# A perceiver block on one core: the steady stage's matmuls in four 64x64 quarters, half sums joined on the way out of PSUM, division behind the Wv products

## The chip, the core and the metric

The kernel runs on one core of a Trainium2 chip. The core has a TensorE (PE in the profile; its weight loads are PEld), a VectorE (DVE), a ScalarE (ACT), a GpSimd (POOL) and a SyncE (SP), which here only issues transfers. Each engine works through its own instructions in a fixed order and waits on semaphores for the others. The metric is the device time in microseconds (us) of one execution, the median of the runs shown. All data is float32.

## The reference, cut to what matters

```python
x = x + xattn(layernorm(x), ctx)      # x: 32 x 64 x 256,  ctx: 32 x 1601 x 192
x = x + time_mixing(layernorm(x))     # a scan over the 64 steps
x = x + ffn(layernorm(x))             # relu, width 1024

def xattn(query, context):            # 16 heads of 64
    q = query @ w_q;  k, v = split(context @ w_kv)
    attn = softmax(q k^T / 8)         # per batch and head, 64 x 1601
    return (attn @ v) @ w_out + b_out

def time_mixing(x):
    k, v, r = ...                     # three 256x256 products of mixes of x and x shifted by a step
    num, den = scans with decay td    # out_t = (num + e v) / (den + e)
    return (sigmoid(r) * out) @ Wo + bo
```

## The kernel before, in words

**Folding.** Keys and values are never formed. A setup stage multiplies each head's query with that head's key weights, so that a query becomes a vector of 192 numbers that is matched with the context itself; the folded queries go to DRAM (`q_dram`) and come back batch by batch. The other way round, the softmax weights are multiplied with the context, which gives 192 numbers per query and head, and only then with the head's value weights (`vproj`, the Wv products) and with `w_out` (`yproj`).

**Units.** The steady stage is the loop `for u in range(2 * B)` over 64 units; a unit is one batch and 8 of its 16 heads, so 8 x 64 = 512 columns. The 1601 keys are 12 chunks of 128, a rest of 64, and one odd key that is treated apart (`odd_pd`, `odd_u`, `share`). For unit u the loop does, in program order:

1. `scores(u)`: six pairs of chunks. The contraction of 192 is cut in three steps of 64 rows, and the two chunks of a pair sit in the upper and the lower 64 rows of the array (L658, form 64*128), each with a PSUM bank of its own. ACT copies each pair to `s_sb` (L665), DVE keeps a running maximum `m` (L667 to L677). For even u, the rest's scores (`rest_scores`, L635) come behind the first pair.
2. `max_all`: POOL's all-reduce over the partitions gives `mb` (L684).
3. For the unit before, u-1: `av_lo` (L468), the weights times the context's first 128 channels, two instructions side by side in the two 64-column halves of the array, and `av_hi` (L864), the last 64 channels. `left` (L809, L819) adds the rest's 64 keys in forms of 64*128. During `av_lo` the queue takes in the `fill` of the unit's phase.
4. `exps(u)`: DVE subtracts `mb` (L692, three L703), ACT exponentiates (L693, three L704).
5. `total(u-1)`, which program order puts ahead of `scores(u)`: DVE sums the exponentials (L766 to L770), POOL all-reduces the sum over the partitions to `den` (L772). `inverse`: DVE turns it (L784), takes the reciprocal of 16 numbers per partition (L786) and turns it back to full width, `rden` (L788, in the buffer of `den`).
6. `before.out()`, for u-2: DVE multiplies `o_lo` and `o_hi` from PSUM with `rden` into `oT_lo` (L885) and `oT_hi` (two L890 of 64 partitions).

**Phases.** Four units are two batches, 128 rows of `x_sb`. So work that belongs to 128 rows goes by the phase (u-5) % 4: phase 0 does `vproj` (L919, L933) behind `av_hi`, and the mixing's `scan` (DVE: eight L575, then L580, L583, a reciprocal L586, L588); phase 1 `yproj` and the mixing's `out` as fills of `av_lo`, and `norm`, whose square root is a POOL power (L111); phase 2 `mix` (transposes L514; ACT and DVE take turns on L523 and L526); phase 3 `project` (Wk, Wv) and `gate` (Wr). In phases 0 and 2 DVE also turns the next batch's context (L372, L373).

**PSUM.** `ps_s` holds two pairs of banks for scores, `ps_o` one bank each for `o_lo` and `o_hi`, `ps_m` two banks for all else. So scores wait for nothing but ACT's copy of the pair two before, and `o_lo` and `o_hi` may stay in their banks until the next unit's `av_lo`.

**Order.** Each engine's order is fixed when the program is built; `tc.issue_after` ties some of it. After the loop there are the last unit, the last mixing and four blocks of the feed-forward net (`ffn`).

Of the kernel before, what the change touches and what calls it, by code (L numbers as in the profile page):

```python
# [9 lines left out]
F32 = mybir.dt.float32  # L10
# [10 lines left out]
def kernel(  # L21
# [51 lines left out]
    ODD = C2 + H  # L73
# [21 lines left out]
    bias_rows = const.tile([P, 3, D], F32, name="bias_rows")  # L95
# [7 lines left out]
    rows = [const.tile([P, 3, P], F32, name=f"rows_{k}") for k in range(2)]  # L103
    odd_pd = const.tile([ODD, 2, P], F32, name="odd_pd")
    odd_u = const.tile([ODD, D], F32, name="odd_u")
    for t in rows + [odd_pd, odd_u]:
        nc.gpsimd.memset(t, 0.0)
# [18 lines left out]
    with ExitStack() as st_b:  # L126
        with ExitStack() as st_a:
# [20 lines left out]
            def rows_load(b):  # L148

                for r0 in (0, C2):  # L150
                    for n, cs in ((0, slice(0, P)), (1, slice(P, C))):
                        nc.sync.dma_start(
                            rows[b % 2][r0 : r0 + KR, n, n * C2 : P], ctx_768[b, KC * P : NK - 1, cs]
                        )
# [282 lines left out]
            def late_loads():  # L437
# [11 lines left out]
                for n, v in enumerate((b_out, bo, b2)):  # L449
                    nc.sync.dma_start(bias_rows[:, n, :], v.partition_broadcast(P))  # L450
                with nc.allow_non_contiguous_dma(reason="per-channel vectors"):
                    for n, v in enumerate((time_decay, time_first)):
                        nc.sync.dma_start(cols[:, n, :], v.rearrange("(c p) -> p c", p=P))
                    for n, v in enumerate((mix_k, mix_v, mix_r)):
                        nc.sync.dma_start(
                            cols[:, 2 + n, :], v.rearrange("a b (c p) -> p (a b c)", p=P)
                        )
                    nc.sync.dma_start(b1_sb, b1.rearrange("(c p) -> p c", p=P))

            ps_m = st_b.enter_context(tc.tile_pool(name="ps_m", bufs=2, space=PSUM))  # L460
            ps_s = st_a.enter_context(tc.tile_pool(name="ps_s", bufs=2, space=PSUM))
            ps_o = st_a.enter_context(tc.tile_pool(name="ps_o", bufs=1, space=PSUM))

            def matmul(out, lhsT, rhs, start, stop):
# [7 lines left out]
                return last  # L472

# [22 lines left out]
            class Mixing:  # L496
# [13 lines left out]
                def mix(self):  # L510
                    i = self.i
                    pt = bank([P, 2, 2, T], f"xT_ln2_{i}")
                    for c in range(2):
                        nc.tensor.transpose(pt[:, c, :, :], self.xn[:, c * P : (c + 1) * P], ident)  # L514
                    xp = rp.tile([P, 2, 2, T + 1], F32, tag="xp", name=f"xp_{i}")
                    nc.gpsimd.memset(xp[:, :, :, 0:1], 0.0)
                    nc.scalar.copy(xp[:, :, :, 1 : T + 1], pt)
# [14 lines left out]
                def proj(self, n, w):  # L532
                    ps = bank([P, 2, 2, T], f"{w}_ps_{self.i}")
# [11 lines left out]
                def project(self):  # L545
# [3 lines left out]
                    pv = self.proj(1, "Wv")  # L549
                    self.ek = rp.tile(shape, F32, tag="in_k", name=f"ek_{i}")  # L550
# [9 lines left out]
                    self.values = nc.vector.tensor_tensor(self.ev, self.e, pv, ALU.mult)  # L560
                def gate(self):
                    i = self.i
                    pr = self.proj(2, "Wr")
# [29 lines left out]
                def out(self):  # L593
                    i = self.i
                    py = bank([P, D], f"ry_{i}")
                    for c in range(2):
                        matmul(
                            py,
                            lhsT=self.rw[:, c, :],
                            rhs=rw_T["Wo"][:, c, :],  # L600
                            start=(c == 0),
                            stop=(c == 1),
                        )
                    nc.vector.tensor_tensor(x_sb[:, i, :], x_sb[:, i, :], py, ALU.add)
                    nc.vector.tensor_tensor(
                        x_sb[:, i, :], x_sb[:, i, :], bias_rows[:, 1, :], ALU.add
                    )

            def rest_scores(b, cT, q):
# [8 lines left out]
                for j in range(2):  # L618
                    rest = ap.tile([P, 2, HH], F32, tag="rest", name=f"rest_{b}_{j}", bufs=3)
                    for o in range(2):  # L620
                        r0 = (1 - o) * KR
                        h0 = j * NP + o * NP // 2
                        nc.gpsimd.memset(rest[r0 : r0 + KR, o, :], LOW)  # L623
                        nc.sync.dma_start(
                            rest[r0 : r0 + 1, o, :].rearrange("p (h t) -> p h t", t=T),
                            o_dram[b // QB][h0 : h0 + NP // 2, k, k * T : (k + 1) * T].unsqueeze(0),
                        )
                    rests.append(rest)
                ps = ps_s.tile([P, 2, HALF], F32, tag="s", name=f"rest_ps_{b}")
                for s in range(NS):  # L630
                    for j in range(2):
                        rs = slice(j * C2, (j + 1) * C2)
                        for o in range(2):
                            n0 = j * HALF + o * HH
                            nc.tensor.matmul(  # L635
                                ps[o * KR : (o + 1) * KR, j, 0:HH],
                                lhsT=cT[rs, s, NB1 * BL : KT],
                                rhs=q[rs, s, n0 : n0 + HH],
# [4 lines left out]
                for j in range(2):  # L643
                    for o in range(2):
                        rs = slice(o * KR, (o + 1) * KR)
                        nc.scalar.copy(rests[j][rs, o, :], ps[rs, j, 0:HH])
                return [r.rearrange("p o n -> p (o n)") for r in rests]

            def scores(u, cT, q, hooks):
# [3 lines left out]
                for i in range(KC // 2):  # L653
                    ps = ps_s.tile([P, 2, HALF], F32, tag="s", name=f"s_ps_{u}_{i}")
                    for s in range(NS):
                        for k in range(2):
                            rs = slice(k * C2, (k + 1) * C2)
                            done = nc.tensor.matmul(  # L658
                                ps[:, k, :],
                                lhsT=cT[rs, s, i * P : (i + 1) * P],  # L660
                                rhs=q[rs, s, js : js + HALF],
                                start=(s == 0),
                                stop=(s == NS - 1),
                            )
# [5 lines left out]
                    if i == 4:  # L670
                        nc.vector.tensor_tensor(m2[:, 1, :], m2[:, 1, :], rests[u % 2], ALU.max)
# [15 lines left out]
            def exps(u, s_sb, rest, mb):  # L687
# [3 lines left out]
                def left():  # L691
                    nc.vector.tensor_tensor(rest, rest, mb, ALU.subtract)  # L692
                    nc.scalar.activation(rest, rest, AF.Exp)  # L693
                    for o in range(2):
                        r, h0 = (1 - o) * KR, j * NP + o * NP // 2
                        nc.scalar.dma_start(
                            pd_dram[b, 0, h0 : h0 + NP // 2].rearrange("h t -> (h t)").unsqueeze(0),
                            rest[r : r + 1, o * HH : (o + 1) * HH],
# [49 lines left out]
            class Half:  # L748
# [14 lines left out]
                def total(self):  # L763
                    u, p = self.u, self.s_sb
                    t2 = aw.tile([P, 2, HALF], F32, tag="t2", name=f"t2_{u}")
                    nc.vector.tensor_tensor(t2, p[:, 0:2, :], p[:, 2:4, :], ALU.add)  # L766
                    nc.vector.tensor_tensor(t2[:, 0, :], t2[:, 0, :], self.rest, ALU.add)
                    for i in range(2, KC // 2):
                        nc.vector.tensor_tensor(t2, t2, p[:, 2 * i : 2 * i + 2, :], ALU.add)  # L769
# [6 lines left out]
                def inverse(self):  # L776
# [5 lines left out]
                    u = self.u  # L782
                    turned = aw.tile([P, HALF // BL, BL], F32, tag="turned", name=f"turned_{u}")
                    nc.vector.transpose(turned, self.den.rearrange("p (k q) -> p k q", q=BL))  # L784
                    few = aw.tile([P, HALF // BL], F32, tag="few", name=f"few_{u}")
                    nc.vector.reciprocal(few, turned[:, :, 0])  # L786
                    self.rden = aw.tile([P, HALF // BL, BL], F32, tag="den", name=f"rden_{u}")
                    nc.vector.transpose(  # L788
                        self.rden, few.unsqueeze(2).to_broadcast([P, HALF // BL, BL])
                    )  # L790

                def keep(self):
# [3 lines left out]
                        self.rden.rearrange("p k q -> p (k q)")[0:1],  # L796
                    )

# [431 lines left out]
```

## Time and profile before

| | us |
|---|---|
| median of 3 runs (lowest, highest) | 2552.46 (2551.37, 2556.37) |
| the profiled execution, span from first to last instruction | 2552.2 |
| first score matmul of a unit to the next one's, phases 0, 1, 2, 3 | 34.93, 38.55, 32.66, 36.42 |
| busy: PE, DVE, ACT, POOL | 2531.5, 1929.0, 982.0, 411.2 |
| scores L658; `o_lo` L468; `o_hi` L864 (busy) | 1008.1; 679.1; 337.0 |
| rest into `o_lo` L809; into `o_hi` L819 (busy) | 81.1; 81.1 |

The span of the profiled execution stands 0.3 us under the median, so that differences against either are the same. In the tables, a row such as "64*128 64x512" is a matmul with 64 rows and 128 columns of the array in use, and 512 columns streamed through 64 partitions. A float32 matmul stands in the trace as two instructions, so counts there are twice those in the code. Four units, phases 0 to 3, are called a cycle here; in the middle of the run a cycle takes 142.56 us.

### The profile page before, as it was taken

The page shows a single profiled execution, that of the slowest core. Times are in us where ns is not written, and L with a number is a line of the kernel's source. Part 1 is how long each engine was busy: PE and PEld are TensorE (multiplying, and loading weights), DVE is VectorE, ACT ScalarE, POOL GpSimd, SP SyncE. Part 2 cuts the span into 40 slices and gives each one's busy share as a digit, 9 for nine tenths or more (in the row PEclk, how much of TensorE's full clock was granted, in tenths as well). Part 3 has the DMA queues.
Part 4 walks back from the last instruction along what each step waited for, and adds up shares of the span by engine and source line. Part 5 has one row for each costly group of instructions (what it writes and reads, how often), then busy time and mean ns, then how long its engine had stood idle before and what let it go on. Part 6 is the DMA issues. An engine that isn't in the chain of part 4 may idle for free.

```text
span 2552.2 us, 38114 instructions
## 1 busy us (share of the span) xinstructions
PE 2531.5 (99%) x15594; PEld 1213.1 (48%) x15594; DVE 1929.0 (76%) x2370; ACT 982.0 (38%) x1097; POOL 411.2 (16%) x372
## 2 busy tenths in 40 slices
PE   9989999999999999999999999999999999999999
PEld 3334444444444444444444454444444444444466
DVE  5377878878787878878787878878787878877741
ACT  3343434434333434434333444343443344343321
POOL 1002111111111121111111111111111111111100
PEclk9999999999999999999999999999999999999999
DMA  8787333333232223233332323233332323310111
GB/s 197 219 211 115 60 67 55 59 66 65 57 66 58 51 55 66 48 66 66 63 62 60 59 42 66 48 66 66 66 66 53 67 41 59 60 34 21 53 46 37
DMA packets 450223, 177.37 MB, mean 69 GB/s; under 512 B 347680, under 2 KB 435776, under 8 KB 450048
## 3 DMA queue, kind: packets, MB, share of 16 engines
q1 hardware_dynamic: 449664, 174.68, 33.5%
q8 instruction: 122, 2.00, 0.4%
q14 instruction: 53, 0.43, 0.1%
q10 hardware_dynamic: 384, 0.26, 0.0%
HBM read 142.64 MB, written 30.67 MB: 68 GB/s over the span
## 4 chain that ended last, share of the span: by engine, by line
PE 92%; DVE 4%; issue 1%; DMA 1%; POOL 1%; ACT 1%; SPq 0%; DVEq 0%; ACTq 0%; POOLq 0%
PE s_ps L658 36%; PE o_lo L468 24%; PE o_hi L864 12%; PE y_ps L468 2%; PE q_ps L292 2%; PE h_ps L1134 2%; PE fy L1150 2%; PE rest_ps L635 2%; PE o_hi L819 1%; PE v_ps L919 1%; PE ql_ps L313 1%; DVE s_sb L703 1%; PE o_lo L809 1%; DVE m L669 1%; PE v_ps L933 1%
## 5 line engine op out<-in xcount | busy, mean ns | idle before, releaser
L658 PE MATMUL s_ps<-q,cT 64*128 64x512 f32 x4608 | 1008.1, 590 | 1.8 <-ACT q_hi L350 0.8
L658 PEld LDWEIGHTS s_ps<-q,cT 64*128 64x128 f32 x4608 | 443.5, 187 | 516.0 <-issue 497.7
L468 PE MATMUL o_lo<-s_sb,c 128*64 128x512 f32 x3024 | 679.1, 596 | 5.9 <-DMA c<-in_ctx_dram 5.9
L665 ACT COPY s_sb<-s_ps 128x1024 f32<-128x1024 f32 x384 | 388.3, 1011 | 739.5 <-PE s_ps L658 731.4
L703 DVE TENSOR_TENSOR s_sb<-s_sb,mb 128x2048 f32<-128x2048 f32 x192 | 431.6, 2285 | 0.0
L704 ACT ACTIVATE s_sb<-s_sb 128x2048 f32<-128x2048 f32 x192 | 367.0, 1912 | 124.3 <-DVE s_sb L703 122.7
L468 PEld LDWEIGHTS o_lo<-s_sb,c 128*64 128x64 f32 x3024 | 209.3, 137 | 387.8 <-issue 383.5
L669 DVE TENSOR_TENSOR m<-m,s_sb 128x1024 f32<-128x1024 f32 x256 | 312.4, 1220 | 40.4 <-ACT s_sb L665 18.2
L864 PE MATMUL o_hi<-s_sb,c 128*64 128x256 f32 x3024 | 337.0, 379 | 0.0
L769 DVE TENSOR_TENSOR t<-t,s_sb 128x1024 f32<-128x1024 f32 x256 | 312.0, 1219 | 8.6 <-DVE t L769 0.5
L864 PEld LDWEIGHTS o_hi<-s_sb,c 128*64 128x64 f32 x3024 | 217.3, 137 | 136.0 <-issue 36.0
L772 POOL PARTITION_ALL_REDUCE den<-t x64 | 207.1, 3236 | 408.0 <-issue 382.4
L784 DVE STREAM_TRANSPOSE turned<-den 128x512 f32<-128x512 f32 x64 | 45.5, 711 | 275.4 <-POOL den L772 275.4
L693 ACT ACTIVATE rest<-rest 128x512 f32<-128x512 f32 x64 | 40.4, 631 | 406.4 <-DVE rest L692 364.1
L684 POOL PARTITION_ALL_REDUCE mb<-m x64 | 114.2, 1785 | 431.9 <-DVE m L677 431.9
L692 DVE TENSOR_TENSOR rest<-rest,mb 128x512 f32<-128x512 f32 x64 | 44.3, 693 | 108.0 <-POOL mb L684 107.9
L623 POOL MEMSET rest<- 64x256 f32 x128 | 39.2, 307 | 412.9 <-PE o_lo L809 326.8
L372 DVE STREAM_TRANSPOSE cT<-cb 128x768 f32<-128x768 f32 x96 | 89.5, 957 | 0.0
L667 DVE TENSOR_TENSOR m<-s_sb 128x1024 f32<-128x1024 f32 x64 | 77.6, 1213 | 9.1 <-ACT s_sb L665 9.1
L111 POOL TENSOR_TENSOR rstd_ln<-rstd_ln,root 128x1 f32<-128x1 f32 (+1 forms) x24 | 33.6, 1402 | 310.7 <-DVE rstd_ln L110 310.7
L809 PE MATMUL o_lo<-rest,rows 64*128 64x256 f32 x252 | 81.1, 402 | 0.0
L819 PE MATMUL o_hi<-rest,rows 64*128 64x256 f32 x252 | 81.1, 402 | 0.0
(165 smaller groups left out, 1823.6 us busy)
## 6 DMA issues: line engine op xcount, KB each, us to landing
q<-q_dram SPq DMA_DIRECT2D x64, 768.0 KB
c<-in_ctx_dram SPq DMA_DIRECT2D x32, 1152.0 KB
cb<-in_ctx_dram SPq DMA_DIRECT2D x192, 104.0 KB
cb<-in_ctx_dram SPq DMA_DIRECT2D x192, 96.0 KB
q_dram<-q_lo SPq DMA_DIRECT2D x16, 1024.0 KB
q_dram<-q_hi SPq DMA_DIRECT2D x16, 512.0 KB
rows<-in_ctx_dram SPq DMA_DIRECT2D x64, 32.0 KB
rest<-o_dram SPq DMA_DIRECT2D x128, 1.0 KB
```

The lines of the kernel that those rows point to most:

```text
L468: last = nc.tensor.matmul(out[rs], lhsT=lhsT[:, rs], rhs=rhs, start=start, stop=stop, skip_group_check=True,)
L658: done = nc.tensor.matmul(ps[:, k, :], lhsT=cT[rs, s, i * P : (i + 1) * P], rhs=q[rs, s, js : js + HALF], start=(s == 0), stop=(s == NS - 1),)
L665: copied = nc.scalar.copy(s_sb[:, 2 * i : 2 * i + 2, :], ps)
L669: nc.vector.tensor_tensor(m2, m2, s_sb[:, 2 * i : 2 * i + 2, :], ALU.max)
L684: nc.gpsimd.partition_all_reduce(mb, mx, P, bass_isa.ReduceOp.max)
L703: nc.vector.tensor_tensor(s, s, m, ALU.subtract)
L704: nc.scalar.activation(s, s, AF.Exp)
L769: nc.vector.tensor_tensor(t2, t2, p[:, 2 * i : 2 * i + 2, :], ALU.add)
L772: nc.gpsimd.partition_all_reduce(self.den, t2[:, 0, :], P, bass_isa.ReduceOp.add)
L809: nc.tensor.matmul(self.po[:, k * HH : (k + 1) * HH], lhsT=self.rows[lo, 0, :], rhs=self.rest[lo, k * HH : (k + 1) * HH], start=(k == 0), ...
L819: nc.tensor.matmul(self.ph, lhsT=self.rows.rearrange("p n c -> p (n c)")[hi, c0 : c0 + P], rhs=self.rest[hi, (1 - k) * HH : (2 - k) * HH], ...
L864: nc.tensor.matmul(self.ph[o * C2 : (o + 1) * C2, :], lhsT=self.ctx[:, self.at[c], P:C], rhs=self.s_sb[:, c, o * HH : (o + 1) * HH], start ...
```

## The change

All of the steady stage's matmuls but Wk, Wv and Wr (and the setup and the last stage) go through the array's four 64x64 quarters. A helper issues four instructions, one for each half of the contraction and each half of the output's partitions. Two halves of a contraction can't share a PSUM bank, so each product has two banks with a half sum each:

```diff
+            def quarters(outs, lhsT, rhs, start, stop):
+                for o in range(2):
+                    for r in range(2):
+                        last = nc.tensor.matmul(
+                            outs[r][half[o]], lhsT=lhsT[half[r], half[o]], rhs=rhs[half[r]],
+                            start=start, stop=stop, skip_group_check=True,
+                        )
+                return last
+            def pair(name):
+                return ps_s.tile([P, 2, HALF], F32, tag="s", name=name)
-            ps_s = st_a.enter_context(tc.tile_pool(name="ps_s", bufs=2, space=PSUM))
-            ps_o = st_a.enter_context(tc.tile_pool(name="ps_o", bufs=1, space=PSUM))
+            ps_s = st_a.enter_context(tc.tile_pool(name="ps_s", bufs=3, space=PSUM))
```

Three pairs of banks now turn over among the scores, the rest's scores, `o_lo`, `o_hi` and the Wv products, in the order in which these are asked for. The half sums are joined when they leave PSUM: ACT copies the one, DVE adds the other.

```diff
+                def joined(self, to, ps):
+                    nc.scalar.copy(to, ps[:, 0].rearrange("p (h t) -> p h t", t=T))
+                    return nc.vector.tensor_tensor(
+                        to, to, ps[:, 1].rearrange("p (h t) -> p h t", t=T), ALU.add
+                    )
+                def out_lo(self):    # self.low = joined(its part of o_lo, self.po)
...
+                def out_hi(self):    # joined(its part of o_hi, self.ph)
...
-                def total(self):
+                def total(self, before=None):
...
+                    with tc.issue_after(before.low.ins) if before else ExitStack():
+                        nc.vector.tensor_tensor(t2, p[:, 0:2, :], p[:, 2:4, :], ALU.add)
...
                     for i in range(2, KC // 2):
+                        if i == 3 and before:
+                            with tc.issue_after(added.ins):
+                                high = before.out_hi()
```

The loop puts `last.out_lo()` between `av_lo` and `av_hi`, ties `share` and `scan` behind it, and moves `vproj` ahead of `av_lo`:

```diff
-                if before is not None:
-                    before.out()
...
+                if phase == 0 and i >= 0:
+                    with tc.issue_after(done.ins):
+                        out.vproj()
                 if last is not None:
                     last.av_lo(fill, done)
...
-                if phase == 0 and i > 0:
-                    older.scan()
                 if last is not None:
+                    last.out_lo()
+                    with tc.issue_after(last.low.ins):
+                        if phase == 0 and i >= 0:
+                            out.share()
+                        if phase == 0 and i > 0:
+                            older.scan()
                     last.av_hi()
-                if phase == 0 and i >= 0:
-                    out.vproj()
```

The division moves: `inverse` stops at the 16 reciprocals (`few`), two transposes per 128 rows widen them (`inverses`), and `vproj` multiplies behind the Wv products, each half of the heads through a pair of banks:

```diff
+                        nc.scalar.copy(self.outT[:, j], pv[:, 0])
+                        nc.vector.tensor_tensor(self.outT[:, j], self.outT[:, j], pv[:, 1], ALU.add)
+                        nc.vector.tensor_tensor(
+                            self.outT[:, j], self.outT[:, j],
+                            self.rden[:, j].rearrange("p h b k q -> p h (b k q)"), ALU.mult,
+                        )
```

`yproj` and the mixing's `out` get both banks of `ps_m`, one per half sum, and DVE adds both; `b_out` rides on a spare row of the odd key's product instead of an addition of its own. `share` now takes a reciprocal of 97x128. The rest's matmuls (`left`) become four of 256 columns behind `av_lo` and four of 128 behind `av_hi`; its heads are laid out in turn instead of in halves, `rows` loses its zeroed columns (a POOL memset per unit) and needs two transfers per batch instead of four. `mix` turns by eight matmuls with a 64x64 identity instead of two transposes. Wr's product uses the unused half of an `o_hi` bank, and `project` issues it.

The order that the built program has on the engines, where the diff doesn't show it: on ACT, the copy out of `o_lo` stands behind the unit's three exponentials L704 and in phase 2 behind the whole of `mix`'s ACT work; on DVE, `out_lo`'s addition closes each unit's block. In phase 0 it is followed by `share`'s reciprocal, the whole `scan` and the first three additions of `total`, and then by `out_hi`'s addition. The scan stands no longer between `total` and the turning of `den`. In phase 1 `yproj`'s two additions stand behind the three subtractions. On TensorE the rest's scores, or for odd u the second pair of scores, wait for `out_lo`'s addition, and the next pair for `out_hi`'s; the mixing's `out` waits for `yproj`'s two additions.

## The prediction

> **What bounds the kernel now.** The page comes first: TensorE is busy all the time and carries the chain that ended last.
>
> ```profile
> PE 2531.5 (99%) x15594; PEld 1213.1 (48%) x15594; DVE 1929.0 (76%) x2370; ACT 982.0 (38%) x1097; POOL 411.2 (16%) x372
> PE 92%; DVE 4%; issue 1%; DMA 1%; POOL 1%; ACT 1%; SPq 0%; DVEq 0%; ACTq 0%; POOLq 0%
> ```
>
> By this, whatever shortens TensorE's queue shortens the run. The table by stage, one cycle from phase 0 to phase 3 and then the whole cycle, shows how near VectorE is (columns: length; busy PE, PEld, DVE, ACT, POOL):
>
> ```profile
> 1014.90:1049.83 34.93, 34.93 (x243) 17.11 (x241) 31.06 (x41) 12.86 (x11) 5.83 (x5) 1.00 0.49 100
> 1049.83:1088.38 38.55, 38.55 (x246) 18.35 (x244) 31.34 (x36) 14.55 (x16) 7.46 (x6) 1.00 0.15 20
> 1088.38:1121.04 32.66, 32.66 (x180) 14.58 (x178) 21.58 (x25) 11.65 (x13) 5.85 (x5) 1.00 0.45 100
> 1121.04:1157.46 36.42, 36.42 (x250) 17.82 (x248) 30.38 (x36) 17.86 (x23) 5.94 (x6) 1.00 0.20 26
> 1014.90:1157.46 142.56, 142.56 (x912) 67.86 (x910) 114.37 (x135) 56.92 (x61) 25.09 (x22) 1.00 0.32 59
> ```
>
> DVE is busy for 114.4 of 142.6 us; 28.2 look free. The waits say what for (total us, times, longest):
>
> ```profile
> DVE turned L784 <- POOL den L772: 275.4, 63, 9.3
> DVE rest L692 <- POOL mb L684: 107.9, 63, 2.0
> DVE m L669 <- ACT s_sb L665: 18.2, 24, 1.4
> ```
>
> The first two are waits for an all-reduce that DVE has itself just fed. Only the third stems from TensorE. The timeline gives the cycle's values of the first:
>
> ```profile
> 1026.17 0.71 DVE L784 STREAM_TRANSPOSE turned<-den 128x512 f32<-128x512 f32 x1 [1.77 <-POOL den L772]
> 1060.12 0.71 DVE L784 STREAM_TRANSPOSE turned<-den 128x512 f32<-128x512 f32 x1 [3.42 <-POOL den L772]
> 1068.19 1.23 DVE L669 TENSOR_TENSOR m<-m,s_sb 128x1024 f32<-128x1024 f32 x1 [0.50 <-ACT s_sb L665]
> 1100.02 0.71 DVE L784 STREAM_TRANSPOSE turned<-den 128x512 f32<-128x512 f32 x1 [9.03 <-POOL den L772]
> 1134.87 0.71 DVE L784 STREAM_TRANSPOSE turned<-den 128x512 f32<-128x512 f32 x1 [3.42 <-POOL den L772]
> ```
>
> So 17.6 us go to `den`, four times 1.5 to 1.9 to `mb`, and 0.5 to TensorE (L669, by way of ACT); the rest are gaps between dependent instructions. DVE and POOL form a ring that takes about 142.1 us a cycle by itself. TensorE bounds the kernel by half a microsecond in 142.6.
>
> **The change part by part: TensorE.** Four quarters run together, as two rows of before show.
>
> ```profile
> 1014.90 15.62 PE L658 MATMUL s_ps<-q,cT 64*128 64x512 f32 x72
> 1041.23 5.35 PE L864 MATMUL o_hi<-s_sb,c 128*64 128x256 f32 x48
> 1052.50 1.53 PE L635 MATMUL rest_ps<-q,cT 64*64 64x256 f32 x24
> L341 PE MATMUL qh_ps<-room,room 64*64 64x512 f32 x128 | 15.7, 602 | 0.1
> L809 PE MATMUL o_lo<-rest,rows 64*128 64x256 f32 x252 | 81.1, 402 | 0.0
> ```
>
> L635 is in quarters already: six groups of four in 1.53 us, and with the last one's 0.38 off, 0.23 per group, the form's switch included. A pair of halves of the same width (L864) takes (5.35-0.38)/23 = 0.216. A group of four costs what a pair costs and does the same work. I take 0.216 for 256 columns, half of it (0.109) for 128 and, from L658, (15.62-0.59)/35 = 0.429 for 512. The upper bound for 512 is L341, 4 x 15.7/128 = 0.49, where short bursts pay for start and end.
>
> A unit then takes 36 groups of scores (15.46), 24 of `o_lo` (10.31), 24 of `o_hi` (5.18) and the rest's two of 256 and two of 128 (0.65; before, two bursts of L809 and L819, 0.53 and 0.54): 31.6. On top come 24 groups of 128 in phase 0 (2.6), 28 of 256 in phase 1 (6.05: rest, `yproj`, `out`), `mix` (0.25), and in phase 3 the rest (1.3) and three products of 0.87 between two switches of form (2.9). The cycle sums to 139.5, so TensorE wins 3.1 of 142.6, mostly changes of form that fall away. Over 14.5 cycles that is 45 us: 2507, if nothing else waits.
>
> **VectorE and ScalarE work.** Removed per cycle: four L788 (0.711 each) and, per unit, two L890 of 0.418 for one addition of the same length: 4.5. Added: two additions and two products of 128x512 behind the Wv products (0.69 each, as L885), two transposes of 1024 per partition (L784 has 0.711 for 512; between that and twice it, I take 1.3), a reciprocal of 97x128 (between L786, 0.251 for 16, and L586, 1.744 for 256: 0.9) and one more addition of 0.41: 6.7. The ring grows by 2.2. ACT gets a copy of 0.58 (as L942) and one of 0.37 (as L646) per unit, 3.8 on 57 busy: covered in sum. SP has two transfers fewer per batch, POOL a memset of 0.2 fewer per unit; both engines idle most of the time, so nothing.
>
> **New waits.** They decide.
>
> *DVE behind ACT.* `out_lo`'s addition needs ACT's copy, which is queued behind the three exponentials. After the last subtraction, ACT has an L704 (1.91) and the copy (0.6) ahead, 2.6 in all with gaps. In phase 0, DVE has 0.4 to do meanwhile and waits 2.2; in phase 3, `ekv` and `ev` cover 0.66 of it: 1.95. In phase 2, `mix` lies between: exponential 1.9, two copies 0.6, then three pairs of L523 (0.7 each) that take turns with DVE's L526 (0.4 until the next pair may start), and the copy: 6.0, less 1.8 of work: 4.2. Before, these turns lay between the subtractions.
>
> *Phase 1, TensorE behind DVE.* `yproj` fills both banks, so the mixing's `out` waits for two additions that stand behind the subtractions. These end about 30 us into the unit (L703 in the old cycle), where TensorE would reach `out` after 27; the stall told below moves both. From the additions on: `out` 0.9, five chunks of `o_lo` 4.3, rest 0.4, copy and gaps 0.9, so 6.5 until `out_lo`'s addition, of which DVE fills 3.4: 3.1.
>
> *`den`.* With the scan gone from that place, the 1.77 becomes a plain 3.42: 1.7 more.
>
> *`out_hi`.* TensorE's delay at `out` makes ACT's copy of `o_hi` late for DVE: about 1.4.
>
> Ring: 142.1 + 2.2 + (2.2+1.95+4.2+3.1) + 1.7 + 1.4 = 158.8. TensorE needs 139.5 and idles 19. Where: in phase 0 DVE's subtractions end 33 us into the unit, `out_lo` is joined at 36.5, and `out_hi`'s addition comes only after `share`, the scan (0.9+0.25+1.6+0.65+0.33+1.7+0.3) and three additions of `total` (1.26+0.62+1.27), 9 us later, at 45.5. TensorE wants that pair 3.9 us into the next unit, at 38: a stall of over 7 in phase 1. Phase 3 has the like: `den` in phase 2 comes after 9 us (the power L111 came before it on POOL, in this phase alone), the subtractions end at 35, and `mix` holds `out_lo` back until 42, while the rest's scores want the banks at 34.5: 7 to 8, and some 2 more at the next pair. Before, `o_lo` and `o_hi` could lie there a whole unit.
>
> Over 14.5 cycles at 16.2 more, plus 3 us at the end, where the last Wv products' additions lie open (two times 0.58+0.69+0.69, some of it beside matmuls): 238. **2552 + 238 gives 2790.** Bounds: were phase 2's long `den` wait only a plain one, 5.6 less per cycle (2709); were the turns of `mix` hidden, 2729, both 2648; with 512 columns at 0.49, the five chunks behind `out` alone add 0.6 per cycle, and phase 0's path, with slack, nothing; with transposes of 1.42 and each new wait longer by a fifth, 2840.
>
> The Trainium skill speaks against the change: "TensorEngine Tiling (Array Packing)", PSUM Bottleneck and Gotcha 1, says that packing speeds up the array but not the way out of PSUM, and that row tiles need banks of their own. The rows above agree with the first half: a group of four is no faster than a pair.
>
> The clock row shows 9 in all 40 slices, with TensorE never idle for long. The Trainium skill, "TensorE: Matmul & The Clock Gate", Part 1, says that about 3.4 us of idling halves the clock until about 3.4 us of work have passed. By that, an estimate from the page is up to 1.7 us lost after each long stall, so at most 49 us if no later stall absorbed it: 2839; by the rows, 2790.
>
> **The rivals.**
>
> *TensorE stays the bound* (faster). The chain view's 92% speaks for it, and DVE's 76%. It needs the joins to come before TensorE asks for the banks, and the ring to stay under 139.5. Time: 2507. Against it, the ring is at 142.1 before anything is added. This is the point from which it decides: every microsecond on the ring over 139.5 is lost.
>
> *The ring grows, but the joins are hidden* (slightly slower): if DVE gets ahead in phases 1 and 3, only work and the `den` wait count: 142.1+2.2+1.7 = 146, 3.5 over: 2604.
>
> *The quarters don't run side by side at 512 columns*, which no steady row shows. At L341's 0.49 the 60 groups of a unit take 3.7 longer, 15 a cycle, and TensorE would need 154, still under the ring's 159, with stalls that only partly overlap: up to 2870.
>
> **How the numbers follow.** The long ring (2790, with its bounds about 2640 to 2840) 0.74; hidden joins 0.10; TensorE as bound 0.12; slow quarters on top of the ring 0.04. The range takes the first and the last and half of the second: 2600 to 2870. A difference of 0.2%, 5 us, is about what a measurement can tell from no change; only the edge between 2507 and 2604 falls within it. Faster 0.12, same 0.02, slower 0.86.
>
> **What would show it.** Right: TensorE's share falls to about 89% (2531-45 busy in 2790); its score matmuls wait for DVE's additions into `oT_lo` and `oT_hi`, some 240 us in total, in phases 1 and 3; the mixing's `out` waits for `yproj`'s additions, some 50; DVE waits for ACT at `oT_lo`; cycles of about 159 us, phases 0 and 2 near 34 and 32. Wrong: cycles under 143, no waits of TensorE for DVE, or groups of four 512-column quarters over 0.45 us apart.

## The result, and the profile after

The changed kernel takes 2818.5 us in the median of four runs (2815.8 to 2819.5), the kernel before 2552.0 (2551.4 to 2556.4): a ratio of 1.104, 95% interval 1.102 to 1.105. The profiled execution took 2815.8 us with a span of 2814.0.

First the page of the changed kernel, with the same two lines that were read before the change:

```profile
PE 2586.0 (92%) x28234; PEld 1225.9 (44%) x28234; DVE 1973.3 (70%) x2370; ACT 1041.1 (37%) x1241; POOL 383.1 (14%) x309
PE 55%; DVE 29%; issue 7%; ACT 5%; POOL 4%; DMA 0%; DVEq 0%; SPq 0%; POOLq 0%; ACTq 0%
```

TensorE had 92% of the chain that ended last and has 55%; DVE had 4% and has 29%. No engine is busy all the time now: time is lost in the handing over.

The table by stage, from phase 0 to phase 3 and then the whole cycle (columns: length; busy PE, PEld, DVE, ACT, POOL; granted clock, DMA share, GB/s):

```profile
1090.67:1124.87 34.20, 34.20 (x456) 16.00 (x452) 28.12 (x29) 13.10 (x13) 5.63 (x4) 1.00 0.36 85
1124.87:1176.32 51.45, 42.10 (x462) 18.08 (x458) 35.94 (x50) 16.03 (x18) 6.23 (x5) 0.90 0.23 27
1176.32:1208.39 32.07, 32.07 (x379) 15.45 (x375) 22.14 (x22) 10.21 (x10) 5.65 (x4) 1.00 0.52 113
1208.39:1251.25 42.86, 37.73 (x435) 17.70 (x431) 31.18 (x35) 21.18 (x31) 5.74 (x5) 0.96 0.10 15
1090.67:1251.25 160.58, 146.10 (x1708) 67.22 (x1704) 117.38 (x135) 60.51 (x70) 23.26 (x18) 0.96 0.28 53
```

A cycle takes 160.6 us and not 142.6. Phases 0 and 2 became a little shorter (34.93 and 32.66 before), as the arithmetic on TensorE promised. Phase 1 took 38.55 and takes 51.45, phase 3 took 36.42 and takes 42.86, and in these two the granted clock is below 1. TensorE's waits in that cycle (total us, times, longest) name the places:

```profile
PE s_ps L483 <- DVE oT_hi L899: 7.2, 2, 6.6
PE rest_ps L669 <- DVE oT_lo L899: 4.5, 1, 4.5
PE ry L483 <- DVE x_sb L1010: 2.8, 1, 2.8
```

The scores of phase 1 wait for the join of `o_hi`, the rest's scores of phase 3 for that of `o_lo`, the mixing's `out` (`ry`) for `yproj`'s additions. All three stand in DVE's queue. What DVE does instead is in its own waits of the same cycle:

```profile
DVE turned L830 <- POOL den L815: 17.1, 4, 6.8
DVE oT_lo L899 <- ACT oT_lo L898: 8.4, 3, 4.6
DVE rest L727 <- POOL mb L718: 6.7, 4, 1.9
DVE in_k L555 <- ACT tmp_k L552: 2.7, 1, 2.7
DVE m L703 <- ACT s_sb L699: 2.2, 3, 1.4
DVE oT_hi L899 <- ACT oT_hi L898: 1.4, 1, 1.4
DVE x_sb L638 <- PE ry L483: 1.2, 1, 1.2
```

117.4 us of work and 39.7 us of these waits make 157.1 of the 160.6; the rest are gaps of half a microsecond and less. Only 3.4 us (L703, L638) are waits for TensorE's own results, and e6 below shows that nearly all of the 4.6 us at `oT_lo` in phase 1 come from TensorE too, by way of ACT's copy. In these places TensorE had itself waited for DVE's additions just before. So DVE is never simply idle although it is busy for 70%: its queue, with its waits, is as long as the cycle.

Over the whole run the sum is: 3.7 us won up to the start of unit 6, 249.2 lost in the 14.25 cycles from there to the last unit, 16.4 lost between the last unit's start and the end (196.7 us there, 180.3 before): 261.9, the difference of the two spans.

### The profile page after: what moved, and what is told of

It reads as the page before. It is cut to its first block, busy times and chain, and to the rows that moved or that the text cites. A ratio compares the mean times of both kernels' runs of the same rounds, so it can differ in the third digit from the quotient of the medians.

```text
span 2814.0 us, 63211 instructions
## 1 busy us (share of the span) xinstructions
PE 2586.0 (92%) x28234; PEld 1225.9 (44%) x28234; DVE 1973.3 (70%) x2370; ACT 1041.1 (37%) x1241; POOL 383.1 (14%) x309
## 4 chain that ended last, share of the span: by engine, by line
PE 55%; DVE 29%; issue 7%; ACT 5%; POOL 4%; DMA 0%; DVEq 0%; SPq 0%; POOLq 0%; ACTq 0%
PE s_ps L483 25%; DVE s_sb L739 12%; PE o_lo L483 11%; PE o_hi L876 5%; DVE m L703 3%; ACT s_sb L740 2%; POOL mb L718 2%; PE h_ps L1185 2%; PE q_ps L293 2%; PE fy L1201 2%; POOL den L815 2%; DVE t L812 1%; DVE t L803 1%; PE ry L483 1%; DVE rest L727 1%
## 5 line engine op out<-in xcount | busy, mean ns | idle before, releaser
L483 PE MATMUL s_ps<-q,cT 64*64 64x512 f32 x9216 | 1051.0, 607 | 101.4 <-DVE oT_hi L899 100.6
L483 PE MATMUL o_lo<-s_sb,c 64*64 64x512 f32 x6144 | 721.2, 601 | 5.1 <-DMA c<-in_ctx_dram 5.1
L483 PEld LDWEIGHTS s_ps<-q,cT 64*64 64x64 f32 x9216 | 371.2, 137 | 722.0 <-issue 582.3
L483 PEld LDWEIGHTS o_lo<-s_sb,c 64*64 64x64 f32 x6144 | 268.2, 136 | 384.7 <-issue 359.5
L703 DVE TENSOR_TENSOR m<-m,s_sb 128x1024 f32<-128x1024 f32 x256 | 313.3, 1224 | 58.4 <-ACT s_sb L699 39.5
L876 PE MATMUL o_hi<-s_sb,c 64*64 64x256 f32 x6144 | 351.2, 376 | 0.0
L876 PEld LDWEIGHTS o_hi<-s_sb,c 64*64 64x64 f32 x6144 | 252.0, 133 | 85.6 <-ACT er L604 0.5
L830 DVE STREAM_TRANSPOSE turned<-den 128x512 f32<-128x512 f32 x64 | 45.5, 711 | 261.1 <-POOL den L815 261.1
L899 DVE TENSOR_TENSOR oT_lo<-oT_lo,o_lo 128x512 f32<-128x512 f32 x64 | 44.0, 687 | 126.5 <-ACT oT_lo L898 124.8
L669 PE MATMUL rest_ps<-q,cT 64*64 64x256 f32 x768 | 66.3, 491 | 62.7 <-DVE oT_lo L899 61.0
L727 DVE TENSOR_TENSOR rest<-rest,mb 128x512 f32<-128x512 f32 x64 | 44.3, 693 | 106.2 <-POOL mb L718 106.2
L669 PEld LDWEIGHTS rest_ps<-q,cT 64*64 64x64 f32 x768 | 34.8, 170 | 99.5 <-DVE oT_lo L899 79.2
```

The source lines that it names most:

```text
L483: last = nc.tensor.matmul(outs[r][half[o]], lhsT=lhsT[half[r], half[o]], rhs=rhs[half[r]], start=start, stop=stop, skip_group_check=True,)
L669: nc.tensor.matmul(ps[half[o], j, 0:HH], lhsT=cT[rs, s, NB1 * BL : KT], rhs=heads[:, :, o, :], start=(s == 0), stop=(s == NS - 1), skip_gr ...
L703: nc.vector.tensor_tensor(m2, m2, s_sb[:, 2 * i : 2 * i + 2, :], ALU.max)
L876: nc.tensor.matmul(self.ph[half[o], r, :], lhsT=self.ctx[half[r], self.at[c], P:C], rhs=self.s_sb[half[r], c, o * HH : (o + 1) * HH], star ...
```

## The experiments

Theory A is the prediction's: DVE's queue, with its waits for POOL and ACT, is the ring that sets the cycle; TensorE's stalls are its shadow. Rival B: the stalls for held PSUM banks set it by themselves, so whatever frees a bank earlier brings its stall's time back. Each kernel is the changed one with the edit shown. `issue_after(x)` means: on x's engine, behind x.

**e1. The join of `o_hi` ahead of the scan.**

```diff
-  with tc.issue_after(last.low.ins):      # behind out_lo
-      out.share(); older.scan()
   last.av_hi()
   ...
   def total(self, before, extra):         # in the next unit
       ... high = before.out_hi()
+      with tc.issue_after(high.ins): share(); scan()
       ... the last three additions
```

> The changed kernel with `share` and the scan moved behind `out_hi`'s addition on DVE (ahead of the last three additions of `total`), nothing else: o_hi's banks come free some 5.7 us earlier in phase 0, DVE's work and its wait for `den` stay. Theory A (DVE with its waits is the ring that sets the cycle): only DVE's own waits behind TensorE's stall go, 2.2 us at L703 in phase 1, so 14.5 x 2.2 = 32 off 2818: about 2786. Rival B (TensorE's stalls for held banks set it): the stall of 6.6 us before the scores of phase 1 and some 2.2 us of half clock behind it go, 14.5 x 8.8 = 128: about 2690.

Measured: 2813.4 us, 5 us less. TensorE's waits over the whole run (100.6, 61.0 and 41.0 us in the changed kernel):

```profile
PE ry L483 <- DVE x_sb L1013: 130.4, 15, 9.6
PE rest_ps L669 <- DVE oT_lo L902: 61.8, 15, 4.7
PE s_ps L483 <- DVE oT_hi L902: 20.2, 20, 1.9
```

The stall before the scores is nearly gone, 100.6 to 20.2, and has come back whole at `ry`, 41.0 to 130.4. The three sum to 212 us; before the edit they summed to 203. This is what a shadow does, and B is out by 120 us. A's own 32 were not had either: DVE's waits for scores fell by 26 us (39.5 to 13.2), but phase 3 gave back what phase 1 won (medians of phases 1 and 3: 49.8 and 44.4 us, without the edit 51.5 and 42.7). The steady cycle takes 160.4 us in both kernels (sums of the four medians); of the two profiled executions, whose spans differ by 2.7 us, e1's is 3.7 us shorter in the first cycle alone. What carries the gain of phase 1 over to phase 3 was not followed further.

**e2. The same work under DVE's wait for `den`.** `share` and the scan stand behind the last addition of `total`.

> As the run before it, but with `share` and the scan behind the last addition of `total`, so that they fill DVE's wait of 3.4 us for `den`. Theory A: 3.4 + 2.2 = 5.6 us a cycle less, 14.5 x 5.6 = 81: about 2737. Rival B: the banks come free no earlier than in the run before: about 2690, as there; by B the two runs are equal, by A they differ by some 49 us.

Measured: 2777.2 us, 41 less. The waits for `den` fell from 261.1 to 211.7 us. The banks of `o_hi` come free no earlier than in e1, yet the run is 36 us shorter; by B the two had to be equal, by A they had to differ by 49. A's own figure, 81 less, was had by half; where the other half went was not followed.

**e3. The context's transposes under the wait for `den`.**

```diff
   last.total(before)
+  if j == 1: with tc.issue_after(last.sum.ins): cT_next = ctx_prep(b + 1)
   ...
-  if j == 0: cT_next = ctx_prep(b + 1)    # came among the maxima
```

> The changed kernel with the context's transposes (L373, L374: 3.25 us twice a cycle) moved on DVE to just behind the last addition of `total` in phases 0 and 2, where DVE waits 3.4 us or more for `den`; no bank, no join and no instruction of TensorE is touched. Theory A: 6.5 us a cycle less, 14.5 x 6.5 = 94: about 2724. Rival B: within 10 us of 2818.

Measured: 2764.8 us, 54 less. DVE's waits for `den` over the whole run, in the changed kernel and in e3:

```profile
DVE turned L830 <- POOL den L815: 261.1, 63, 7.2
DVE turned L830 <- POOL den L815: 171.8, 63, 4.0
```

Nothing of TensorE or PSUM was touched, and B, which asked for no change, is out a second time. TensorE's three stalls fell as well, from 203 to 171 us, since the joins came earlier: they follow DVE's queue. A asked for 94: the waits for `den` did fall by 89 us (to 171.8), but 29 came back because the transposes had been covering other waits (for `mb` 106.2 to 120.6, for scores 39.5 to 45.8, for `oT_lo` 124.8 to 132.9).

**e4. POOL's fill behind the all-reduce.**

```diff
-  nc.gpsimd.memset(rest[...], LOW)
+  with tc.issue_after(dens[-2].ins) if j == 0 ...:   # behind den's all-reduce
+      nc.gpsimd.memset(rest[...], LOW)
```

> The changed kernel with POOL's fill of the first `rest` tile queued behind the all-reduce of `den` and not ahead of it. In phase 2 that fill waits for o_hi's last product until 1177 us, and the all-reduce starts only 7.7 us after it has been passed, though its operand is there after 5. Theory A: after a power on POOL the all-reduce needs about 7.5 us of preparation, which can now begin right behind the power; DVE's wait in phase 2 falls from 6.8 to 3.4, 14.5 x 3.4 = 49: about 2769. Rival: the preparation begins only when the operand comes, or is not tied to the fill: no change, or even 4 us a cycle more (2818 to 2876).

Measured: 2769.0 us, 49.5 less, and DVE's longest wait for `den` is 3.5 us where it was 7.2. POOL's timeline, first of the changed kernel, then of e4 (start, duration, what ended the idle time before):

```profile
1164.96 0.60 POOL L115 TENSOR_TENSOR rstd_ln<-rstd_ln,root 128x1 f32<-128x1 f32 x1 [9.14 <-DVE rstd_ln L114]
1177.16 0.67 POOL L653 MEMSET rest<- 64x256 f32 x2 [11.60 <-issue]
1185.73 3.25 POOL L815 PARTITION_ALL_REDUCE den<-t  x1 [7.91 <-issue]
```

```profile
1148.55 0.60 POOL L115 TENSOR_TENSOR rstd_ln<-rstd_ln,root 128x1 f32<-128x1 f32 x1 [9.15 <-DVE rstd_ln L114]
1165.71 3.25 POOL L815 PARTITION_ALL_REDUCE den<-t  x1 [16.56 <-PE s_ps L483]
1169.02 0.67 POOL L653 MEMSET rest<- 64x256 f32 x2
```

Its operand is DVE's last addition of `total`, again first in the changed kernel, then in e4:

```profile
1181.51 0.69 DVE L813 TENSOR_TENSOR t<-t 128x512 f32<-128x512 f32 x1
1164.81 0.69 DVE L813 TENSOR_TENSOR t<-t 128x512 f32<-128x512 f32 x1
```

In the changed kernel the all-reduce starts 7.9 us after the fill, which had to wait for `o_hi`'s last product, although its operand was ready at 1182.2. Moved ahead of the fill, it starts 0.2 us after its operand (1165.5). So in phase 2 the all-reduce needs some 7.9 us of preparation, which lies hidden unless an instruction in between holds the queue. That the power is what calls for it fits the runs, since L115 stands ahead of this all-reduce alone, but none left the power out.

**e5. Mix's blending behind the join of `o_lo`.**

```diff
   last.out_lo()
+  with tc.issue_after(last.half.ins), tc.issue_after(last.low.ins):
+      mixer.blend()       # L552 and L555, so far in the fill of av_lo
```

> The changed kernel with the blending of `mix` (ACT's L552, DVE's L555) queued behind `out_lo`'s copy and addition in phase 2; mix's products and its copies out of PSUM stay where they are. Theory A: DVE's waits of 3.7 us at L555 go and one of about 2.0 at oT_lo comes, 14.5 x 1.7 = 25 off 2818: about 2793. Rival B (TensorE's stalls set the time): oT_lo comes 5 us earlier, so the stall of 4.5 us before the rest's scores in phase 3 goes, with 0.6 at the next pair and some 1.3 us of half clock: 14.5 x 6.4 = 93: about 2725.

Measured: 2790.9 us, 28 less: A's figure. TensorE's waits show once more how little a stall says by itself:

```profile
PE s_ps L483 <- DVE oT_hi L900: 128.0, 30, 6.9
PE rest_ps L670 <- DVE oT_lo L900: 20.4, 15, 2.0
```

The rest's scores wait 41 us less, and the next scores 27 us more.

**e6. `out` in spare halves of `o_hi`'s banks.**

```diff
-  py = [bank([P, D], f"ry_{i}_{r}") for r in range(2)]
+  py = last.spares        # high[:, r, HH:HALF]
```

> The changed kernel with the mixing's `out` written into the unused halves of the two banks of `o_hi`, as `project` does with its gate, and not into the pair that `yproj` has just filled; `out` no longer waits for DVE's additions of `yproj`. Theory A: TensorE is no longer held up at `out`, so in phase 1 DVE's wait at oT_lo falls from 4.6 to 2.0 and those at x_sb (1.2) and oT_hi (1.4) go: 14.5 x 5.2 = 75: about 2743. Rival B: TensorE's 2.8 us and about 1 us of half clock: 14.5 x 3.8 = 55: about 2763. Rival C (another wait takes its place, as the one at `out` did for the one at the scores when `out_hi` was moved up): within 15 us of 2818.

Measured: 2765.2 us, 53 less. Rival C is out. B's figure is hit (2763) and A's missed by 22: DVE's waits at `oT_lo` fell from 124.8 to 63.9 and those at `x_sb` went, as A said, but it waited 11 us more for scores and 8 more at `oT_hi`. This run does not tell A from B.

**e7. All five** (e2 to e6).

> The changed kernel with five edits at once: scan and `share` under the wait for `den`, the context's transposes under the wait for `den`, the fill of `rest` behind the all-reduce, mix's blending behind `out_lo`, `out` in the spare halves. If the gains add up (41, 54 and 49 measured, 25 and 75 expected) 2818 - 244 = 2574, slightly over the kernel before. If DVE's chain then falls below TensorE's own 139.2 us a cycle: 2507. If each one's cover is used up by the others: not under 2650.

Measured: 2620.4 us, ratio to the kernel before 1.027 (1.025 to 1.029). 198 of the 226 us that the five had brought singly. The 2574 that full addition gave is missed by 46 us, 22 of them because e6 had brought 53 and not 75. One large wait of TensorE is left, and it is a child of e6:

```profile
PE o_hi L878 <- DVE x_sb L639: 63.2, 14, 5.5
```

`o_hi`'s own products wait until `out`'s additions, behind the subtractions on DVE, have read the same banks.

**e8. A control on the kernel before.** The transposes as in e3, and a fourth buffer of `rest` in place of e4's order.

> A control on the kernel before: the context's transposes under the wait for `den` (6.5 us a cycle off DVE's queue) and a fourth buffer of `rest`, so that POOL's fill no longer holds the all-reduce back (up to 5.6 us a cycle). Theory A: TensorE alone bounds that kernel by half a microsecond a cycle: 2545 to 2552. Rival: if DVE's ring already sets the time before, 2552 - 14.5 x 6 = about 2465.

Measured: 2551.8 us, ratio 0.9996 (0.9987 to 1.0005). DVE's waits for `den` and POOL's rows in phases 2 and 3 show what the two edits did; the second view is the kernel before in phase 2:

```profile
DVE turned L784 <- POOL den L772: 233.8, 63, 7.3
1086.46 0.66 POOL L623 MEMSET rest<- 64x256 f32 x2 [4.19 <-issue]
1094.31 3.25 POOL L772 PARTITION_ALL_REDUCE den<-t  x1 [7.19 <-issue]
1127.10 3.23 POOL L772 PARTITION_ALL_REDUCE den<-t  x1 [3.86 <-issue]
```

```profile
1088.78 0.66 POOL L623 MEMSET rest<- 64x256 f32 x2 [4.18 <-issue]
1096.74 3.25 POOL L772 PARTITION_ALL_REDUCE den<-t  x1 [7.29 <-issue]
```

The fourth buffer did not do what it was meant to: in phase 2 the fill still comes 4.2 us behind the power, and the all-reduce 7.2 us behind the fill. So the control tests the transposes alone. They took 41.6 us off the waits for `den` (275.4 before), while DVE's waits for scores grew by 14.8 (18.2 to 33.0) and those for `mb` by 12.8 (107.9 to 120.7), and a steady cycle takes 142.56 us in both. What is worth 54 us in the changed kernel is worth nothing in the kernel before: there TensorE bounds. For e4's order there is no such control.

**e9. All five, and `out` in phase 0 of the next cycle.**

```diff
+  elif phase == 0 and i > 1: fill = {6: [mixers[i - 2].out]}   # own banks again
-  6: [lambda: older.out(last.spares)]                          # phase 1
-  self.rw = rp.tile(..., tag="xn")
+  self.rw = num           # the scan's quotient stays there until then
```

> The kernel with all five edits, and `out` of the tile before moved from phase 1 into phase 0 of the next cycle, into banks that nobody has filled since; the scan's quotient stays in `num` until then. In the run with five edits the only stall of TensorE left was o_hi of phase 1 behind the additions of `out` (63 us in 14 stalls, with about 1.7 us of half clock behind each). Theory A: with that gone TensorE alone bounds the kernel, at about 34.2 + 0.9, 37.7, 31.8 and 36.5 us, 141.1 a cycle against 142.6 before: 2620 - 14 x 5.6 = about 2540, 0.5% under the kernel before. Rival: DVE's chain still sets phase 1, and the stall returns at another place: 2600 or more.

Measured: 2548.6 us (2540 expected), ratio 0.9984 (0.9975 to 0.9993): 0.16% under the kernel before. Its cycle, from phase 1 to phase 0, and the whole:

```profile
1037.85:1074.40 36.55, 36.55 (x449) 18.09 (x442) 33.02 (x44) 14.76 (x16) 6.87 (x5) 1.00 0.01 3
1074.40:1106.37 31.97, 31.97 (x376) 22.91 (x374) 25.99 (x26) 13.73 (x15) 5.65 (x4) 1.00 0.72 130
1106.37:1143.84 37.47, 36.10 (x435) 17.36 (x429) 29.65 (x34) 17.46 (x26) 5.73 (x5) 1.00 0.01 2
1143.84:1178.90 35.06, 35.06 (x473) 16.61 (x468) 30.67 (x34) 14.46 (x14) 5.62 (x4) 1.00 0.61 120
1037.85:1178.90 141.05, 139.68 (x1709) 74.97 (x1704) 119.32 (x135) 60.42 (x70) 23.88 (x18) 1.00 0.32 61
```

TensorE is full again, the clock is whole, and DVE does even more work (119.3 us) than in the changed kernel: no operation was removed; what changed is the order, and the buffers that `out` and the scan's quotient use. The steady cycle is 1.5 us shorter than before, but 13 of the 16 us lost behind the last unit are still there (span 2546.2, last unit at 2352.8: 193.4), so little of it reaches the end.

**e10 and e11. Halves in place of quarters**, in the changed kernel and in e9.

```diff
-  for o in range(2):
-      for r in range(2): matmul(outs[r][half[o]], lhsT[half[r], half[o]], rhs[half[r]])
+  for r in range(2): matmul(outs[r], lhsT[half[r]], rhs[half[r]])
```

> The changed kernel with every group of four quarters that L483 issues (scores, o_lo, yproj, the mixing's out) replaced by two halves of 64 rows x 128 columns, into the same two banks, with the same joins; half as many matmul instructions there. Theory A: the form of the product is nothing to the time, what costs is the two banks and their joins: 2818, within 15. Rival C (quarters run slower than halves at 512 columns, or their number of instructions costs): 60 groups a unit at 0.06 us, 52 us or more less: under 2770.

> The kernel of the first of these three runs with L483's products in halves, as in the second. Theory A says that TensorE alone bounds it, so that what quarters are worth in themselves shows here: the changes of form between halves and quarters that come back, some eight in a cycle at 0.15 us, are 1.2 us a cycle, 17 us more than the first run: about 2557. Rival: with half the instructions the sequencer is faster: not over 2540.

Measured: 2829.5 us (11 more than the changed kernel) and 2574.9 (26 more than e9, 18 more than expected). So the 266 us are not the price of the quarters: halves that fill the same two banks pay them too (`o_hi`, the rest and the Wv products stay in quarters in both runs). Quarters are worth 26 us, 1.0%, where TensorE bounds. Why is shown only in part: TensorE is busy for 2542.5 us with halves and 2492.8 with quarters, 3.0 us a cycle. In the traces a cycle has about 20 places where the form changes from one TensorE instruction to the next with halves, and 6 with quarters. At the 0.15 us of the expectation, which no row here gives, these 14 make 2.1 us; a run for the changes alone is missing. Units of phases 0 to 3 take 35.06, 36.55, 31.97 and 37.47 us with quarters (the last with its stall of 1.4) and 35.79, 37.83, 32.53 and 36.57 with halves.

**e12. A last wait, and a miss.** On top of e9, mix's copies and blending move into phase 3, DVE's part under the wait for `den`; at the end, joins go ahead of the norms.

> The kernel with `out` in phase 0, and two more orders changed: mix's copies out of PSUM and its blending move from phase 2 into phase 3, ACT's behind the copy of o_hi and DVE's under the wait for `den` (the one of the four that nothing filled yet); and at the end of the attention DVE's joins, the scan and yproj's additions go ahead of the norms of the last stage. Theory A: the last stall in the cycle, 1.4 us of phase 3's scores behind oT_hi, goes with what it drags along, 37.46 becomes 36.5: 14.5 x 1.0 = 14; at the end the stalls of 2.2, 4.3 and 3.5 us behind oT_lo, outT and x_sb shrink by about 5 together: 2548.6 - 19 = about 2530, 0.9% under the kernel before. Rival (TensorE's queue needs the 141 us by itself): 2544 to 2550.

Measured: 2623.3 us, ratio 1.028 (1.026 to 1.029), 75 more than e9. ACT's timeline in phase 3, and the one long wait of TensorE:

```profile
1147.97 0.69 ACT L554 ACTIVATE tmp_v<-xp,omm 128x128 f32<-128x128 f32 x2 [5.89 <-DVE in_k L557]
1148.57 0.73 ACT L681 COPY rest<-rest_ps 64x256 f32<-64x256 f32 x2
```

```profile
PE s_ps L483 <- ACT rest L681: 77.9, 14, 6.2
```

ACT's second blending step needs the buffer that DVE's first one reads. With DVE's part put off to the wait for `den`, ACT stood 5.9 us in front of the rest's copy, and that copy frees the bank that the next scores want. Both engines' places had to be weighed, and only DVE's was. The other half of the edit did work: from the last unit's start to the end this run takes 186.6 us where e9 takes 193.4, 6.8 less (about 5 were expected). The miss lies in phase 3 alone, which takes 43.2 us and not 37.5.

## Why the prediction was right, and where it was off

It said 2790 (2600 to 2870); the time is 2818.5. Its mechanism, a ring through DVE's queue that outgrows TensorE, is what the runs show. That the number came so close is partly luck, since errors offset each other. By the spans, 261.9 us were lost and 238 forecast: 14 more in the cycles, 13 more at the end, 4 fewer at the start. By its own steps:

- **TensorE alone.** 139.5 us a cycle were predicted. The changed kernel never shows it undisturbed; e9 does, with 139.7 busy us at full clock; with the scores and `o_lo` in halves (e11) a cycle takes 142.7, so the 3.1 us that the sum won are there. A group of four 512-column quarters costs 0.43 us in the steady stage, as the neighbour row of halves said, not the 0.49 of the short bursts: the changed kernel's row below has six groups, and without the last one's 0.59 it gives 2.16/5. The prediction took it as agreeing with half of what is said of packing that a group of four is no faster than a pair. It bears on neither half: both forms fill the whole array, and neither row holds a way out of PSUM. What the way out costs is shown by the runs that move the joins and the work beside them, e1 to e9.

```profile
1124.87 2.75 PE L483 MATMUL s_ps<-q,cT 64*64 64x512 f32 x24
```

- **The ring of 158.8.** The cycle is 160.6, and e1, e2, e3 and e8 show that the ring sets it: the order of the joins alone moves the stall and hardly the time, what fills DVE's own waits moves the time, and the transposes moved in the kernel before do nothing. The 160.6 hold 3.4 us of waits for TensorE at L703 and L638, where the sum had 0.5 taken out as TensorE's; without them the ring is 157.2. Its terms: work +3.0 (2.2 predicted; DVE was busy 114.4 us a cycle and is 117.4). Waits at `out_lo` 2.0, 1.8 and, with mix between, 3.7 in phases 0, 3 and 2 (2.2, 1.95 and 4.2). In phase 1 4.6, not 3.1. `den` in phase 1 3.4, as predicted; `out_hi` 1.4, as predicted.
- **`den` in phase 2** was taken at its old 9.0; it is 6.8. The step kept the duration and did not ask what the preparation runs beside. e4 shows what: the fill of `rest`. These 2.2 us too many covered most of the 2.9 us of waits for TensorE that the sum left out.
- **Where TensorE idles.** The places were right (scores behind `oT_hi` in phase 1, rest behind `oT_lo` in phase 3, `ry`), the sizes too large: 6.6, 4.5 and 2.8 us, 203 us in all and not 290; TensorE's busy share is 92% and not 89%. The missing part is the next point.
- **The clock.** The sum took full clock. TensorE was busy for 2586.0 us at a mean clock of 0.960, in e9 for 2492.8 with the same 28234 instructions at 0.995: 93 us more, most of it half clock. The estimate from the Trainium skill ("TensorE: Matmul & The Clock Gate", Part 1) was at most 49 and counted two long stalls a cycle. This trace shows why it was too low; the last section has the numbers: in the cycle shown, TensorE works for 4.6, 3.4 and 2.8 us at half clock, and half of their sum is 5.4 of the 6.4 us by which its busy time exceeds e9's. How much of the 93 us lengthened the run can't be told from these runs: DVE's ring accounts for the cycle nearly without it, so most of it probably only filled time in which TensorE would have stalled longer.
- **The end.** 3 us were allowed; 16.4 were lost. The joins of the last unit, the scan and the norms of the next stage share DVE's queue there, and `yproj` waits 3.4 us and the second Wv group 3.8 for joins. This is the term that was plainly mis-sized, and with 28 us between forecast and time it is half of the difference. e12, which changes the order there, gets 6.8 us back against e9.
- **The early cycles** were summed like all others. The first, in which the mixing's scan and `out` do not yet take part, took 150.5 us against 141.8 before: +8.7, not +16.

## What to carry to other kernels

An engine that is busy for three quarters can already be the whole cycle: add its waits for what it has itself just fed, and a change that gives it more to do, or puts it behind another engine's queue, costs that much at once, whatever the array gains. Where a stall is only a shadow, freeing its bank moves it elsewhere, while filling the bounding engine's own waits shortens the run; a control on the kernel before tells which of the two one has. When an instruction is moved into such a gap, look also at the other engine that it feeds or whose buffer it holds.

## What the hardware showed that was not expected

**A stall of 2.77 us was enough to halve the clock.** The granted clock around phase 1's stall of 6.58 us, around the stall of 2.77 us at `ry`, and at both ends of the half clock that follows phase 3's stall of 4.5 us (window, length, busy PE, clock, DMA):

```profile
1130.90:1132.90 2.00, 0.00 (x0) 1.00 1.58 137
1132.90:1133.90 1.00, 0.00 (x0) 0.69 1.60 122
1133.90:1135.50 1.60, 0.00 (x0) 0.50 0.66 84
1135.50:1139.50 4.00, 3.99 (x20) 0.50 0.00 0
1139.50:1140.50 1.00, 1.00 (x12) 0.69 0.00 0
```

```profile
1160.80:1163.50 2.70, 0.00 (x0) 1.00 0.00 0
1163.50:1164.50 1.00, 0.96 (x6) 0.75 0.00 0
1164.50:1165.50 1.00, 1.00 (x15) 0.50 0.00 0
1166.50:1167.50 1.00, 1.00 (x12) 0.54 0.00 0
```

```profile
1215.00:1215.50 0.50, 0.00 (x0) 0.71 0.00 0
1218.50:1219.00 0.50, 0.15 (x4) 0.88 1.16 183
```

A value between 0.5 and 1 tells where in its window the clock changed. After the long stall the clock is at half from about 1133.3 to 1140.1, 6.8 us, of which TensorE works through 4.6. After the short one it is at half from about 1164.0 to 1167.4, 3.4 us, all of them work: the gate fell when TensorE was already at work again. After phase 3's it is at half from about 1215.2 to 1218.6, again 3.4 us. The stretches are two, one and one times 3.41 us long, and the second and the third begin 9 and 24 such lengths after the first. So the gate seems to judge fixed windows of this length by how idle they were on the whole: the one that ends at 1164.0 was idle for 2.77 of its 3.41 us. The same section of the Trainium skill says that an idle window of about 3.4 us halves the clock and that the window runs freely. The trace agrees with the second; as to the first, a window that was idle for four fifths was enough. A stall of under 3 us can thus cost some 1.7 us more, an estimate from 3.4 us of work at half clock.

**An all-reduce behind a power on POOL starts late.** The one in phase 2 is the only one with a power ahead of it since the last all-reduce. It starts 7.3 us (before), 7.2 (e8) and 7.9 (changed) after the fill, and in the changed kernel 3.5 us after its operand. In phase 3, with no power ahead, it has started 3.9 us after the fill (e8). In e4, with nothing between the two, that time lies beside other work. No run left the power out.
